# A two-layer relational graph network: copying two tiles of rows in every eighth chunk instead of every sixteenth

## The chip, the cores and the metric

The kernel runs on one core of a Trainium2 chip. Its engines are TensorE (PE, matrix products), VectorE (DVE), ScalarE (ACT), GpSimd (POOL) and SyncE (SP). ACT, POOL and SP each also have a queue in which they start memory transfers, written ACTq, POOLq and SPq in the profile. The metric is the time of one execution in microseconds, the median of several runs. Lower is better.

## The reference

There are 50,000 nodes with 128 features each and 850,000 edges, of which 50,000 go from a node to itself. The edges are sorted by the node that they end in. Each edge has one of 16 types, and each type's matrix is a mix of 8 basis matrices. Two layers of this kind run one after the other, then comes a residual and a normalisation:

```
def _rgcn_layer(h, src, dst, rel, basis, w_comp, loop_w, bias):
    W = jnp.einsum('rb,bio->rio', w_comp, basis)
    seg = dst.astype(jnp.int32) * N_REL + rel.astype(jnp.int32)
    agg = jax.ops.segment_sum(h[src], seg, num_segments=N_ENT * N_REL)
    agg = agg.reshape(N_ENT, N_REL, -1)
    msg = jnp.einsum('nri,rio->no', agg, W)
    out = msg + h @ loop_w + bias
    return jax.nn.relu(out)
...
x = _layernorm(x + layer2(layer1(x)), axis=-1)
```

For every edge the 128 numbers of its source node have to be fetched: `h[src]`. These are 512-byte rows at places that are known only when the kernel runs.

## The kernel before

**Chunks.** The 800,000 edges that are not self-loops are cut into 625 chunks of 10 tiles of 128 edges (`C`, `K`, `P`). The loop over `c` near line 1238 goes through the chunks, once for each layer. The rows of one tile come with one indirect transfer that GpSimd starts (`gather`, line 270): 128 rows into the 128 partitions of one slice of a buffer `g`. In layer 1 there are four buffers of ten tiles and the gathers of chunk c+2 are written beside the products of chunk c (`FETCH`). In layer 2 there are nine buffers (the later ones are named `d_r`, `k_loop`, `real_both`, `full` and `parts`), and the gathers of chunk c+7 stand there.

**Products.** VectorE makes a matrix `hot` for each chunk (lines 1099 and 1106) that says, for every edge, to which of the next 30 nodes and with which of the 8 basis weights it counts. TensorE multiplies the fetched tile with it into a bank of PSUM (line 1273), five tiles to a bank, and VectorE adds the bank to `ring` (line 1130), which holds the sums of three groups of 512 nodes. When a group is finished, ScalarE copies its sums out (`own`, line 915), TensorE multiplies them with the basis (line 919), ScalarE applies the relu (line 934), and the result is turned back and stored.

**The copied tiles.** Some tiles are not gathered by GpSimd. For a chunk in `copied_rows` the gather of tile 9 (`COPIED`) is left out, and SyncE or ScalarE fetches the 128 rows one by one with 128 direct transfers of 512 bytes. The class `Copied` does this. `load` fetches the 128 row addresses from DRAM (line 1181). `copy` loads 16 of them at a time into the engine's registers (line 1190, shown as TENSOR_LOAD; the 128th alone on line 1188), computes each address (line 1191, shown as FUSED_REGOPS or ISA) and starts the transfer (line 1192). Before the change each of the two engines does this for every sixteenth chunk (`EVERY`), with one buffer each.

**What sets the order.** Work that is not part of the chunk's own products stands in a list of events with a due time. One unit of due time, called a slot below, is one tile's product, so that a chunk is ten slots. `later(time, ...)` enters an event, and `go_on(now)` writes out what is due after each product. The rows of a copied tile are such events: `planned` spreads the 128 of them over a stretch of slots ahead of the chunk. TensorE takes the copied tile of chunk c at slot 10c+5, as the first tile of the second half. The engines PE, POOL, DVE and ACT execute in the order in which the program is written (line 1093). SP is not in that list before the change, so its order is chosen by the framework's scheduler.

**Semaphores of the transfers.** The transfers of SyncE and ScalarE together tell of their landing with eight semaphores, DMAHW0 to DMAHW7, which are handed out in turn. Each transfer waits until the one before it on the same semaphore has landed. That is the eighth transfer before it, counted over both queues.

Of the kernel before, what the change touches and what calls it, by code (L numbers as in the profile page):

```python
# [40 lines left out]
F32 = mybir.dt.float32  # L41
# [10 lines left out]
P = 128  # L52
# [4 lines left out]
K = 10  # L57
# [15 lines left out]
GATHERS = 4  # L73
J = 4
AHEAD = 16
EACH = 2 * len(WINDOWS)
NEAR = 128
BATCH = 4
# [9 lines left out]
WIDE = 1  # L88
PARTS_OF = ((0, 3), (3, 5))
EPS = 1e-5  # L90
EVERY = 16
COPIED = 9
EARLY = ((27, 35), (19, 27))
LEAD = 2
AT_A_TIME = 16

# [6 lines left out]
def tile_rgcn_resnorm(  # L103
# [55 lines left out]
    consts = ctx.enter_context(tc.tile_pool(name="consts", bufs=1))  # L159
    col = consts.tile([P, P], F32, name="col")  # L160
    nc.gpsimd.iota(col, pattern=[[1, P]], base=0, channel_multiplier=0, allow_small_or_imprecise_dtypes=True)
    part = consts.tile([P, 1], F32, name="part")
    nc.gpsimd.iota(part, pattern=[[0, 1]], base=0, channel_multiplier=1, allow_small_or_imprecise_dtypes=True)
    ident = consts.tile([P, P], F32, name="ident")
    nc.vector.tensor_scalar(ident, col, part, None, op0=OP.is_equal)

    single = consts.tile([P, 4], F32, name="single")
    eps, apart_by, odd, ones = (single[:, i : i + 1] for i in range(4))
    nc.vector.memset(eps, EPS)

# [12 lines left out]
    def weighed(brief):  # L183
# [19 lines left out]
        for n, (basis, w_comp, loop_w, bias) in enumerate(GIVEN):  # L203
            ec = brief.tile([P, NB], F32, name="ec")
            nc.scalar.dma_start(
                ec, bass.AP(tensor=w_comp.tensor, offset=w_comp.offset, ap=[[0, AT], [NB, NR], [1, NB]])
            )
            nc.vector.tensor_tensor(
                each[:, n],
                ec[:, None, :].to_broadcast([P, AT, NB]),  # L210
                one_tile[:, :, None].to_broadcast([P, AT, NB]),
                op=OP.mult,
            )

            column_of = consts.tile([P, 1], F32, name=f"bias_of{n}")
            nc.scalar.dma_start(column_of, bass.AP(tensor=bias.tensor, offset=bias.offset, ap=[[1, P], [1, 1]]))
            BIAS_OF.append(column_of)
            left, mine = ec, brief.tile([P, NB], F32, name="mine")
            for i in range(PARTS):
                short = brief.tile([P, NB], BF16, name=f"short{i}")  # L220
                nc.vector.tensor_copy(short, left)
                if i == 0:
                    nc.vector.tensor_scalar(mine, short, which[:, i : i + 1], None, op0=OP.mult)
                else:
                    nc.vector.scalar_tensor_tensor(
                        mine, short, which[:, i : i + 1], mine, op0=OP.mult, op1=OP.add
                    )
                if i + 1 < PARTS:
                    less = brief.tile([P, NB], F32, name=f"less{i}")
                    nc.vector.tensor_tensor(less, left, short, op=OP.subtract)  # L230
                    left = less
            nc.vector.tensor_copy(split[:, n], mine)
# [483 lines left out]
    def chunked():  # L716
        with (
# [334 lines left out]

            def indexed(n, b, copy):
                first_of, end_of = b * AHEAD * K, min(C, (b + 1) * AHEAD) * K
                index[n, b] = hp.tile([P, AHEAD * K], I32, name="index", bufs=3)
                return copy(index[n, b][:, : end_of - first_of], src[:, first_of:end_of])

            placed = indexed(0, 0, nc.vector.tensor_copy)
# [31 lines left out]
                for who, engine in enumerate((nc.sync, nc.scalar))  # L1090
            ]
            ordered = ExitStack()
            ordered.enter_context(tc.manual_schedule(engines={mybir.EngineType.PE, mybir.EngineType.Pool, mybir.EngineType.DVE, mybir.EngineType.Activation}))
            for n, of in enumerate((x, H1)):

                def hot_of(c):
# [17 lines left out]
                def places(c):  # L1114
                    loaded_for[0] = n, c // BATCH
                    some = min(BATCH, C - c) * EACH
                    which_of = c % AHEAD // BATCH * BATCH * EACH
                    nc.vector.load(at_reg[:some], offs[c // AHEAD][0:1, which_of : which_of + some])

                def add(c, half, i, pa):  # L1120

# [30 lines left out]
                offs = {}  # L1152

                def offsets(b):
                    first_of, end_of = b * AHEAD * EACH, min(C, (b + 1) * AHEAD) * EACH
                    offs[b] = hp.tile([1, AHEAD * EACH], I32, name="offs")
                    nc.sync.dma_start(
                        offs[b][:, : end_of - first_of], OFF[first_of:end_of].rearrange("(p k) o -> p (k o)", p=1)
                    )
# [12 lines left out]
                class Copied:  # L1172
# [3 lines left out]
                        self.order = [*range(1, P), 0]  # L1176

                    def load(self):
                        self.to = hp.tile([P, D], F32, name=f"copied{self.who}", bufs=1)
                        self.away = self.to.bitcast(I32)[0:1, :]  # L1180
                        nc.sync.dma_start(self.away, AWAY[2 * self.c + 1 : 2 * self.c + 2])

# [12 lines left out]
                        )  # L1195

                    def planned(self, queue):
                        begin = K * (self.c - EVERY + LEAD) + PER
                        queue(begin - K, self.load)
                        for i in range(P):  # L1200
                            queue(begin + i * (EVERY - 2 * LEAD) * K // P, self.copy, i)

                copied_rows = {
                    c: Copied(c, who) for who, early in enumerate(EARLY[n]) for c in range(early, C, EVERY)
# [4 lines left out]
                batches = [Weights(c, n) for c in range(0, C, BATCH)]  # L1209
                batches[0].load()  # L1210
                offsets(0)
                for b in range(1, -(-C // AHEAD)):
                    later(K * AHEAD * b - K, offsets, b)
                if n == 0:
                    batches[0].compare()
                    batches[0].multiply()
# [13 lines left out]
                for one in groups:  # L1230
                    free = one.planned(later, free)
                if n:
                    with tc.issue_after(back[0].ins):
                        matrices(1, nc.sync)

                into = rows + more_rows(pr) if n else rows
                ahead = FETCH[n]
# [272 lines left out]
```

## Time and profile before

| | |
|---|---|
| median of 3 runs | 15,544.52 us (15,542.33 to 15,545.87) |
| the profiled execution | 15,567.63 us; span from the first to the last instruction 15,565.8 us |
| busy: PE / DVE / ACT / POOL | 62% / 50% / 11% / 75% of the span |
| POOL instructions | 12,390 |
| copied tiles | 151: 76 by SyncE, 75 by ScalarE |
| memory traffic | 98 GB/s over the span, DMA engines about a third busy |

The page of the profile gives busy time by engine, the span in 40 slices, the chain of work that ended last, and groups of instructions. A group's row names the line, the engine, the operation and the tiles, then after the bar its busy time in us, the mean of one in ns, and the idle time of the engine just ahead of it. A trace can be asked further for one tile's or line's instructions (shortest, median and longest in ns), for who waited for whom (us in total, times, longest), for stretches of time, and for the instructions in order of time.

### The profile page before, as it was taken

To read this page: it belongs to the slowest core of one execution; us is meant where nothing else is said; L and a number is where in the kernel's file an instruction comes from. 1 tells how busy PE (TensorE), PEld (TensorE's weight loads), DVE (VectorE), ACT (ScalarE), POOL (GpSimd) and SP (SyncE) were. 2 spreads that over 40 slices of the span, in tenths; PEclk is the share of its full clock that TensorE was granted. 3 is DMA by queue.
4 is the path that set the end of the run, shared out by engine and by line. 5 is a ranking of instruction groups with operands and counts; after the bars stand their busy time and mean duration, and the time that the engine had idled before them with its cause. 6 is when DMAs were issued, how large, how long until landed. Compare 5 with 4: busy or idle time off the path is not lost.

```text
span 15565.8 us, 164019 instructions
## 1 busy us (share of the span) xinstructions
PE 9727.8 (62%) x31567; PEld 7176.4 (46%) x31567; DVE 7738.2 (50%) x11079; ACT 1642.8 (11%) x2031; POOL 11742.7 (75%) x12390
## 2 busy tenths in 40 slices
PE   5666566666666666666666666666666666666666
PEld 4444444444444444444444444444444444444444
DVE  7655555565444444444444444444444444444444
ACT  1111111111111111111100000000000000000000
POOL 7777777777777777777777777777777777777777
PEclk7877887777888888888877777787777777777778
DMA  4333333333333333333333333333333333333332
GB/s 125 109 111 107 109 110 106 107 106 105 99 99 96 99 99 98 98 99 98 94 92 94 94 94 94 93 92 93 94 94 94 94 94 94 92 94 94 94 94 81
DMA packets 827507, 1530.93 MB, mean 98 GB/s; under 512 B 245150, under 2 KB 332937, under 8 KB 826472
## 3 DMA queue, kind: packets, MB, share of 16 engines
q0 software_dynamic: 397104, 817.16, 18.8%
q1 hardware_dynamic: 408424, 697.64, 13.4%
q10 hardware_dynamic: 20944, 5.55, 0.2%
q14 instruction: 778, 6.37, 0.1%
q8 instruction: 257, 4.21, 0.1%
HBM read 1391.28 MB, written 128.09 MB: 98 GB/s over the span
## 4 chain that ended last, share of the span: by engine, by line
POOL 61%; issue 24%; DMA 11%; PE 2%; DVE 1%; SPq 1%; ACTq 0%; ACT 0%; POOLq 0%; DVEq 0%
POOL g L270 43%; DMA g<-in_x_dram,index 5%; POOL d_r L270 4%; POOL k_loop L270 4%; POOL parts L270 4%; POOL full L270 4%; POOL real_both L270 3%; DMA g<-H,index 2%; PE pa L1273 1%; DMA real_both<-H,index 1%; DMA full<-H,index 1%; DMA k_loop<-H,index 1%; DMA parts<-H,index 1%; DMA d_r<-H,index 1%; SPq L1190 0%
## 5 line engine op out<-in xcount | busy, mean ns | idle before, releaser
L1273 PE MATMUL pa<-hot,g 128*128 128x240 f32 x17882 | 5490.0, 459 | 4012.8 <-DMA g<-in_x_dram,index 2195.9
L270 POOL DMA_INDIRECT g<-in_x_dram,index x6175 | 5875.3, 951 | 1890.1 <-issue 1783.7
L1273 PEld LDWEIGHTS pa<-hot,g 128*128 128x128 f32 x17882 | 4155.0, 242 | 5580.4 <-issue 2374.8
L1130 DVE TENSOR_TENSOR ring<-pa,ring 128x240 f32 x5000 | 2038.6, 408 | 7077.2 <-PE pa L1273 6275.3
L1106 DVE TENSOR_TENSOR hot<-pm,fixed 128x2400 f32<-128x2400 f32 x1250 | 3317.9, 2654 | 69.7 <-ACT pm L789 17.4
L270 POOL DMA_INDIRECT g<-H,index x2766 | 2616.6, 946 | 857.1 <-issue 814.1
L919 PE MATMUL pn<-own,basis 128*128 128x512 f32 x3072 | 1808.1, 674 | 0.0
L900 DVE TENSOR_TENSOR ring<-wide,pa 128x2048 f32<-128x2048 f32 (+1 forms) x386 | 876.4, 2270 | 230.8 <-DMA wide<-CW 212.2
L915 ACT COPY own<-ring 128x4096 f32<-128x4096 f32 x192 | 692.3, 3606 | 2444.1 <-DVE ring L1130 1100.6
L270 POOL DMA_INDIRECT k_loop<-H,index x682 | 645.2, 946 | 208.1 <-issue 197.4
L270 POOL DMA_INDIRECT real_both<-H,index x682 | 645.3, 946 | 208.0 <-issue 194.3
L270 POOL DMA_INDIRECT d_r<-H,index x682 | 645.2, 946 | 208.0 <-issue 198.6
L270 POOL DMA_INDIRECT parts<-H,index x681 | 644.3, 946 | 207.8 <-issue 197.4
L270 POOL DMA_INDIRECT full<-H,index x681 | 644.2, 946 | 207.8 <-issue 194.7
L919 PEld LDWEIGHTS pn<-own,basis 128*128 128x128 f32 x3072 | 667.3, 219 | 65.5
L1273 PE MATMUL pa<-hot,real_both 128*128 128x240 f32 x1364 | 445.4, 482 | 334.7 <-DMA real_both<-H,index 317.0
L1273 PE MATMUL pa<-hot,k_loop 128*128 128x240 f32 x1364 | 442.6, 479 | 318.7 <-DMA k_loop<-H,index 287.3
L1273 PE MATMUL pa<-hot,full 128*128 128x240 f32 x1362 | 444.3, 481 | 310.5 <-DMA full<-H,index 292.3
L1273 PE MATMUL pa<-hot,d_r 128*128 128x240 f32 x1364 | 442.6, 479 | 311.7 <-DMA d_r<-H,index 275.2
L1273 PE MATMUL pa<-hot,parts 128*128 128x240 f32 x1362 | 444.4, 481 | 304.1 <-DMA parts<-H,index 268.6
L887 ACT COPY pa<-hT 128x512 f32<-128x512 f32 x392 | 228.8, 587 | 3534.0 <-DMA copied<-H 1798.0
L1099 DVE TENSOR_TENSOR fixed<-fixed,key 128x300 f32<-128x300 f32 x1250 | 584.5, 468 | 1.6
(181 smaller groups left out, 5255.8 us busy)
## 6 DMA issues: line engine op xcount, KB each, us to landing
wide<-CW SPq DMA_DIRECT2D x388, 1024.0 KB
g<-in_x_dram,index POOLq DMA_INDIRECT x6175
copied<-in_x_dram SPq DMA_DIRECT2D x4864, 0.5 KB
copied<-H SPq DMA_DIRECT2D x4864, 0.5 KB
copied<-H ACTq DMA_DIRECT2D x4864, 0.5 KB
copied<-in_x_dram ACTq DMA_DIRECT2D x4736, 0.5 KB
rows<-in_x_dram SPq DMA_DIRECT2D x194, 256.0 KB
g<-H,index POOLq DMA_INDIRECT x2766
```

The source lines that it names most:

```text
L270: return nc.gpsimd.indirect_dma_start(out=to, out_offset=None, in_=of, in_offset=bass.IndirectOffsetOnAxis(ap=idx, axis=0))
L887: nc.scalar.copy(self.laid[b][:, : self.cnt], self.hT[:, : self.cnt])
L900: nc.vector.tensor_tensor(into, wide, laid[:, None, :].to_broadcast([P, AT_ONCE, cnt]), op=OP.mult)
L915: nc.scalar.copy(self.sums, ring[:, :, at : at + cnt])
L919: nc.tensor.matmul(self.pn[:, a:e], BASIS[:, b, :], self.sums[:, b, a:e], start=False, stop=b == NB - 1)
L1099: nc.vector.tensor_tensor(own, grid[:, None, :].to_broadcast([P, K, WN]), key[:, c * K : (c + 1) * K, None].to_broadcast([P, K, WN]), op=O ...
L1106: nc.vector.tensor_tensor(hot, pm[:, c % BATCH * K * NB : (c % BATCH + 1) * K * NB].rearrange("e (k b) -> e k b", b=NB)[:, :, :, None].to_ ...
L1130: nc.vector.tensor_tensor(into, pa[:, before : before + NB * w].rearrange("d (b w) -> d b w", w=w), into, op=OP.add,)
L1273: nc.tensor.matmul(pa[:, before : before + NB * w], fetched, hot[:, half * PER + j].rearrange("e b w -> e (b w)"), start=(i, j) == mine[i][0],
```

## The change

Each engine now copies a tile for every eighth chunk (`EVERY` 8). SyncE starts at chunk 20 in layer 1 and 12 in layer 2, ScalarE four chunks later. Each has two buffers in place of one. The 128 copies of a tile are spread over 80 slots, from slot 10(c-9)+5 to slot 10(c-1)+5; before they were spread over 120 slots, from 10(c-14)+5 to 10(c-2)+5. SyncE's transfers stand in the written order, since SP joins the list of engines with a manual schedule. To make room in SBUF, `index` has two buffers instead of three, the offsets of eight chunks are loaded at once instead of sixteen, and a few one-column constants share a tile. The load of the second layer's matrices no longer names a transfer that it is to follow.

```
+PLACED = 8
...
-EVERY = 16
+EVERY = 8
 COPIED = 9
-EARLY = ((27, 35), (19, 27))
+EARLY = ((20, 24), (12, 16))
...
-                index[n, b] = hp.tile([P, AHEAD * K], I32, name="index", bufs=3)
+                index[n, b] = hp.tile([P, AHEAD * K], I32, name="index")
...
-            ordered.enter_context(tc.manual_schedule(engines={mybir.EngineType.PE, mybir.EngineType.Pool, mybir.EngineType.DVE, mybir.EngineType.Activation}))
+            ordered.enter_context(tc.manual_schedule(engines={mybir.EngineType.PE, mybir.EngineType.Pool, mybir.EngineType.DVE, mybir.EngineType.Activation, mybir.EngineType.SP}))
...
-                    first_of, end_of = b * AHEAD * EACH, min(C, (b + 1) * AHEAD) * EACH
-                    offs[b] = hp.tile([1, AHEAD * EACH], I32, name="offs")
+                    first_of, end_of = b * PLACED * EACH, min(C, (b + 1) * PLACED) * EACH
+                    offs[b] = hp.tile([1, PLACED * EACH], I32, name="offs")
...
-                        self.to = hp.tile([P, D], F32, name=f"copied{self.who}", bufs=1)
+                        self.to = hp.tile([P, D], F32, name=f"copied{self.who}")
...
-                        begin = K * (self.c - EVERY + LEAD) + PER
+                        begin = K * (self.c - EVERY - LEAD + 1) + PER
                         queue(begin - K, self.load)
                         for i in range(P):
-                            queue(begin + i * (EVERY - 2 * LEAD) * K // P, self.copy, i)
+                            queue(begin + i * EVERY * K // P, self.copy, i)
...
-                for b in range(1, -(-C // AHEAD)):
-                    later(K * AHEAD * b - K, offsets, b)
+                for b in range(1, -(-C // PLACED)):
+                    later(K * PLACED * b - 2 * K, offsets, b)
...
-                    with tc.issue_after(back[0].ins):
-                        matrices(1, nc.sync)
+                    matrices(1, nc.sync)
```

(`tc.manual_schedule` keeps the written order on the engines named. The pool `hp` has two buffers where none is named.)

The first place is on POOL, early in layer 1. Each row is one chunk's gathers, with the count behind the x. Before:

```order
L270 DMA g_102<-in_x_dram,index 128x128 x9
L270 DMA g_99<-in_x_dram,index 128x128 x10
L270 DMA g_100<-in_x_dram,index 128x128 x10
L270 DMA g_101<-in_x_dram,index 128x128 x10
L496 DMA FULL<-full,to_i 1638400x2
L270 DMA g_102<-in_x_dram,index 128x128 x10
L270 DMA g_99<-in_x_dram,index 128x128 x10
L270 DMA g_100<-in_x_dram,index 128x128 x10
L270 DMA g_101<-in_x_dram,index 128x128 x10
L270 DMA g_102<-in_x_dram,index 128x128 x9
```

And with the change (its lines are one further down):

```order
L271 DMA g_98<-in_x_dram,index 128x128 x9
L271 DMA g_99<-in_x_dram,index 128x128 x10
L271 DMA g_100<-in_x_dram,index 128x128 x10
L271 DMA g_101<-in_x_dram,index 128x128 x10
L271 DMA g_98<-in_x_dram,index 128x128 x9
L271 DMA g_99<-in_x_dram,index 128x128 x10
L271 DMA g_100<-in_x_dram,index 128x128 x10
L497 DMA FULL<-full,to_i 1638400x2
L271 DMA g_101<-in_x_dram,index 128x128 x10
L271 DMA g_98<-in_x_dram,index 128x128 x9
```

A chunk with nine gathers comes every fourth chunk instead of every eighth. No other POOL instruction moves.

The second place is on SP, in the middle of layer 1, with the semaphores that each row waits for in brackets. L1190 loads sixteen addresses, L1192 starts one row's transfer, and L1191 between them computes the address. Before:

```order
L1192 DMA copied_25547<-in_x_dram 1x128 [waits DMAHW0_49]
L874 DMA wide<-CW 128x4x512 [waits DMAHW1_49,DVE_49]
L755 DMA rel<-REL 128x1x640 [waits DMAHW2_49,DVE_49]
L1191 ISA
L1192 DMA copied_25547<-in_x_dram 1x128 [waits DMAHW3_49]
L1191 ISA
L1192 DMA copied_25547<-in_x_dram 1x128 [waits DMAHW4_49]
L1191 ISA
L1192 DMA copied_25547<-in_x_dram 1x128 [waits DMAHW5_49]
L1191 ISA
L1192 DMA copied_25547<-in_x_dram 1x128 [waits DMAHW6_49]
L1181 DMA copied_26377<-AWAY 1x128 [waits DMAHW7_49,Activation_sequencer_49,PE_49]
```

And with the change, where the same three lines are L1191, L1193 and L1192:

```order
L1193 DMA copied_35952<-in_x_dram 1x128 [waits DMAHW6_49]
L1192 ISA
L1193 DMA copied_35952<-in_x_dram 1x128 [waits DMAHW0_49]
L1192 ISA
L1193 DMA copied_35952<-in_x_dram 1x128 [waits DMAHW2_49]
L1192 ISA
L1193 DMA copied_35952<-in_x_dram 1x128 [waits DMAHW4_49,SP_sequencer_49]
L1191 TENSOR_LOAD copied_37159 [waits DMAHW5_49]
L1192 ISA
L1193 DMA copied_37159<-in_x_dram 1x128 [waits DMAHW5_49]
L1192 ISA
L1193 DMA copied_37159<-in_x_dram 1x128 [waits DMAHW6_49]
```

Before, SP's rows here take the eight semaphores one after the other, so that the transfers between are its own. With the change they take every second one, the others going to ScalarE's rows, and the next tile's load of addresses follows directly on the last row of the tile before.

More of the change, by code (lines that the diff above doesn't have):

```diff
@@ L161, in tile_rgcn_resnorm @@
     nc.gpsimd.iota(col, pattern=[[1, P]], base=0, channel_multiplier=0, allow_small_or_imprecise_dtypes=True)
-    part = consts.tile([P, 1], F32, name="part")
+    single = consts.tile([P, 8], F32, name="single")
+    part = single[:, 4:5]
     nc.gpsimd.iota(part, pattern=[[0, 1]], base=0, channel_multiplier=1, allow_small_or_imprecise_dtypes=True)
@@ L165, in tile_rgcn_resnorm @@
     nc.vector.tensor_scalar(ident, col, part, None, op0=OP.is_equal)
-    single = consts.tile([P, 4], F32, name="single")
     eps, apart_by, odd, ones = (single[:, i : i + 1] for i in range(4))
@@ L213, in weighed @@
             )
-            column_of = consts.tile([P, 1], F32, name=f"bias_of{n}")
+            column_of = single[:, 5 + n : 6 + n]
             nc.scalar.dma_start(column_of, bass.AP(tensor=bias.tensor, offset=bias.offset, ap=[[1, P], [1, 1]]))
```

4 lines of the change are left out of this document (2 added, 2 removed).

## Prediction

> **What bounds the kernel now.** I read the page first: the chain that ended last, then GpSimd's group.
>
> ```profile
> POOL 61%; issue 24%; DMA 11%; PE 2%; DVE 1%; SPq 1%; ACTq 0%; ACT 0%; POOLq 0%; DVEq 0%
> L270 POOL DMA_INDIRECT g<-in_x_dram,index x6175 | 5875.3, 951 | 1890.1 <-issue 1783.7
> ```
>
> The chain is GpSimd's. One gather takes 951 ns and 0.306 us of idle time stand ahead of it, nearly all "issue", which means that it waits for nobody. Then I read stretches of time, one in each layer:
>
> ```profile
> core 0: us, PE busy (x) PEld busy (x) DVE busy (x) ACT busy (x) POOL busy (x), PEclk, DMA share, GB/s
> 5000.00:6000.00 1000.00, 632.76 (x2151) 476.25 (x2150) 463.38 (x555) 113.87 (x136) 755.91 (x800) 0.81 0.33 98
> 11000.00:13000.00 2000.00, 1261.99 (x3790) 912.63 (x3788) 934.66 (x1317) 192.27 (x239) 1512.23 (x1600) 0.78 0.31 94
> ```
>
> GpSimd issues 800 gathers in 1000 us and 1600 in 2000 us: one every 1.250 us, without a pause. No other engine is busy for more than two thirds. There are 2 x 625 x 10 - 151 = 12,349 gathers (the 151 copied tiles are the row of line 1181 below), and 12,349 x 1.250 = 15,436 us. The remaining 130 us of the span are the start, the turn between the layers and the end. A chunk takes 15,436 / 1250 = 12.35 us. In the list of waits there is no row in which PE waits for a copied tile, so today the copies arrive in time.
>
> **What the change removes.** Copied tiles in layer 1: SyncE for chunks 20, 28, ... 620 and ScalarE for 24, ... 624, 76 each. In layer 2: 12, ... 620 and 16, ... 624, 77 each. Together 306, which is 155 more than 151. So 155 gathers go, and if GpSimd stays the bound this is worth 155 x 1.250 = 194 us. Nothing hides them. A chunk would then have 9.75 gathers and take 12.19 us.
>
> **What it adds: 155 x 128 rows on two queues.** Each queue must now deliver 16 rows in each chunk's 12.19 us, all the time. Before it was 16 rows in 1.5 chunks, with a pause of four chunks after each tile. So the question is what 16 rows cost a queue. The copied tile's instructions (shortest/median/longest in ns):
>
> ```profile
> L1192 SPq DMA_DIRECT2D copied<-in_x_dram x4864: 224/228/922, 123.5 to 7688.8; - x195
> L1190 SPq TENSOR_LOAD <-copied x608: 3257/3524/5519, 119.4 to 15326.6; - x152
> L1190 ACTq TENSOR_LOAD <-copied x600: 3212/3738/6103, 304.4 to 15425.0; - x150
> L1188 SPq TENSOR_LOAD <-copied x76: 447/538/806, 247.5 to 15341.3; - x76
> L1181 SPq DMA_DIRECT2D copied<-AWAY x151: 215/231/867, 110.2 to 15287.0; - x151
> ```
>
> 608 loads for 76 tiles are eight for a tile, one for each 16 rows, and one costs the queue 3.5 us (SP) or 3.7 us (ACT). The Trainium skill, in "DMA: Bandwidth & Descriptors", section "Latency and other measured facts", gives a floor of about 600 ns for such a register load; the row for one register (538 ns) agrees, but by that figure alone for 16 registers a batch would be 2.9 us cheaper, the queues would have room to spare and the change would bring its 194 us. The measured load of 16 decides against it.
>
> The pace of rows, from stretches without a wait, in order of time (start, us, ... xcount):
>
> ```profile
> 5058.66 1.46 SPq L1192 DMA_DIRECT2D copied<-in_x_dram  x4
> 5060.22 0.40 SPq L874 DMA_DIRECT2D wide<-CW  x1
> 5060.82 2.69 SPq L1192 DMA_DIRECT2D copied<-in_x_dram  x7
> ```
>
> ```profile
> 5146.71 1.00 ACTq L1192 DMA_DIRECT2D copied<-in_x_dram  x3
> ```
>
> SP: (1.46 - 0.228) / 3 = 0.411 us a row. ACT, with the same 0.23 us for the last: (1.00 - 0.23) / 2 = 0.385 us. Another transfer between SP's rows (`wide`) stretches the gap from 5060.12 to 5060.82, 0.70 us where 0.18 us is usual: its own 0.40 us and 0.12 us around it.
>
> So 16 rows without any wait cost SP 3.52 + 16 x 0.411 + about 0.1 behind the load, and an eighth of the single load (0.08): **10.3 us**. ACT: 3.74 + 16 x 0.385 + 0.2 = 10.1 us, and 0.3 us as an estimate for handing on its own 1.6 instructions a chunk (239 in 2000 us above).
>
> SP also carries all other transfers:
>
> ```profile
> L874 SPq DMA_DIRECT2D wide<-CW x392: 364/399/447, 99.2 to 15445.9; - x196
> L824 SPq DMA_DIRECT2D lrel<-LREL x98: 641/672/692, 81.2 to 7594.8; - x98
> L755 SPq DMA_DIRECT2D rel<-REL x157: 582/629/757, 20.9 to 7689.1; - x157
> L936 SPq DMA_DIRECT2D H1T<-oT x98: 319/354/862, 217.8 to 7815.6; - x98
> ```
>
> In layer 1 there are 196 `wide`, 98 `lrel`, 157 `rel`, four more kinds of 98 and one of 157 at about 0.354, and with the change 152 + 79 short ones at 0.23: 78 + 66 + 99 + 139 + 56 + 53 = 491 us, and 1,231 x 0.12 = 148 us around them: 639 us over 625 chunks, **1.02 us a chunk**. Layer 2 has no `lrel`, `rel` or `CW`: 196 `wide`, three kinds of 98 and one of 157, 154 + 79 short ones, by the same sum 0.64 us.
>
> SP's queue is thus taken for 11.3 of 12.19 us in layer 1 and for 10.9 in layer 2. What is left for waits is 0.9 and 1.3 us a chunk.
>
> **What waits cost.** Each transfer waits for the eighth before it. SP's own list of waits, for the rows alone (us, times, longest):
>
> ```profile
> SPq L1192 <- DMA wide<-CW: 278.3, 98, 4.8
> SPq L1192 <- DMA copied<-in_x_dram: 195.7, 150, 6.3
> SPq L1192 <- DMA copied<-H: 169.5, 179, 4.6
> SPq L1192 <- DMA lrel<-LREL: 55.0, 24, 4.7
> SPq L1192 <- DMA rows<-in_x_dram: 38.9, 32, 5.4
> SPq L1192 <- DMA out_dram<-t: 10.2, 6, 1.8
> ```
>
> Layer 1 has `in_x_dram`, `lrel`, `rows` and half of `wide`: 429 us over its 304 loads, 1.41 us for 16 rows. Layer 2: 319 us, 1.05 us. By these, SP needs 12.7 us a chunk in layer 1, over the 12.19, and 12.0 in layer 2, just under.
>
> The two queues also stop each other, since they share the eight semaphores:
>
> ```profile
> 5124.22 21.09 ACTq L1192 DMA_DIRECT2D copied<-in_x_dram  x16
> ```
>
> ```profile
> 5140.09 0.36 SPq L831 DMA_DIRECT2D rows<-in_x_dram  x1
> ```
>
> These 16 rows of ScalarE took 21.1 us instead of 10.1, and they went on when SyncE had issued its `rows`. That one was SyncE waiting for an engine, which goes away when the queues lag. The part that stays is that with both queues always copying, the eight transfers between are four of each: 4 x 0.411 = 1.64 us, where SP alone has 8 x 0.411 = 3.3. No view gives this part. Below it is 0: each queue's waits fall together. Above, a load of one queue (3.5 us) lets the other go on for eight rows at most, 8 x 0.385 = 3.1 us; losing 0.4 us at each of two loads a batch is 0.8 us. I take 0.3, nearer the lower end since most waits are for `wide` and `lrel`, which hold both queues at once.
>
> **The sum.** Layer 1: 11.3 + 1.4 + 0.3 = 13.0 us a chunk against 12.35: 625 x 0.65 = +406 us. Layer 2: 10.9 + 1.05 + 0.3 = 12.25, against 12.35: -62 us. When the copies are late, PE waits at slot 10c+5 of the copied chunk, its buffers stay full, and GpSimd waits for a buffer: three chunks of gathers ahead cover a single delay, but not a queue that is too slow on average. The profiled time of 15,568 becomes 15,912; the median shown lies 23 us below the profiled execution, so I say **15,890 us**.
>
> The other edits cost nothing that I can find: the written order on SP puts every transfer at its due slot, 10 to 60 slots ahead of its use; `index` is rewritten only when its gathers lie seven chunks or more back; 39 more loads of offsets a layer are in the sum.
>
> **Rivals.** (A) The waits fall where a queue is ahead and would wait anyway; GpSimd stays the bound. For it: no PE wait for a copied tile today, and ten slots (12 us) between the last row's due slot and its use. Against: the queues are 90% taken before any wait. Then 15,545 - 194 = **15,350 us**. (B) The queues run at about today's chunk, 12.35 us on average: no change, 15,545. (C) The forecast: the row copies of SyncE bound layer 1. (D) Full coupling: 0.8 instead of 0.3 us, 13.5 and 12.75 us a chunk, 625 x (1.15 + 0.40) = +970 us, **16,510 us**. It decides as soon as one queue's load regularly stops the other. (E) SyncE, now in written order, stops at a transfer whose data are not there, and rows queue behind it; each such stop over the slack of 12 us would cost its excess. Today's largest sum of that kind is
>
> ```profile
> SPq L1181 <- PE pa L1273: 1812.3, 142, 27.7
> ```
>
> 12.8 us on average, for a buffer that PE has yet to free; with two buffers it was freed a whole tile earlier, so I count this rival to D.
>
> **How the numbers follow.** A 0.35, B 0.06, C 0.42, D and E 0.17. A measurement of this kernel can tell 0.2% (31 us) from no change. Faster is A, slower is C, D and E: 0.35, 0.06, 0.59. The forecast is C's. C's own range, with 0 to 0.6 us of coupling (12.7 to 13.3 and 12.19 to 12.55 us a chunk), is 15,660 to 16,260. The range that holds 8 in 10 reaches from A's full gain to D: 15,340 to 16,450.
>
> **What would show it.** If C is right, the waits of the profile have a new row "PE pa <- DMA copied", GpSimd issues fewer than 800 gathers in 1000 us in layer 1 (about 750) but near 800 in layer 2, GpSimd's idle time is ended by PE, and SP's queue in layer 1 has next to no waits for other engines left. If A is right, 800 in both, and PE never waits for `copied`. If layer 2 is as slow as layer 1, it is D. I would be wrong altogether if a row's transfer or a load took a different time at twice the density; the medians of lines 1191 and 1193 would show it.

## The result and the profile after

The changed kernel takes 16,392.78 us (16,383.57 to 16,406.22) against 15,544.97 us beside it. The ratio is 1.0546, with an interval from 1.0528 to 1.0565. It is slower by 848 us where the prediction said 345. The time lies inside the range of 15,340 to 16,450 us, but above the range of the forecast's own theory C, 15,660 to 16,260. The profiled execution took 16,406.22 us (span 16,404.4), 839 us over that of the kernel before.

Where the time went is read first. The first fence is the answer for the tile `g` on GpSimd, in the kernel before: shortest, median and longest gather in ns, then the first and the last start in us.

```profile
L270 POOL DMA_INDIRECT g<-in_x_dram,index x6175: 943/947/2332, 18.8 to 7805.6; - x200
L270 POOL DMA_INDIRECT g<-H,index x2766: 943/947/1044, 7820.2 to 15543.1; - x198
```

The second is the same for the changed kernel, whose lines are one further down.

```profile
L271 POOL DMA_INDIRECT g<-in_x_dram,index x6098: 938/945/1997, 18.8 to 8609.7; - x197
L271 POOL DMA_INDIRECT g<-H,index x2731: 940/945/1183, 8664.6 to 16304.2; - x196
```

Layer 2 begins at 7,820.2 us before and at 8,664.6 us after, so layer 1 lost 844 us. Layer 2 takes 15,565.8 - 7,820.2 = 7,746 us before and 16,404.4 - 8,664.6 = 7,740 us after: its 77 fewer gathers brought nothing that shows. A gather itself is as long as it was.

The chain that ended last and three groups of the changed kernel (busy us, mean ns, then idle us ahead and who ended most of it):

```profile
SPq 34%; DMA 28%; issue 13%; ACTq 12%; POOL 5%; DVE 3%; PE 3%; ACT 1%; DVEq 0%; POOLq 0%
L271 POOL DMA_INDIRECT g<-in_x_dram,index x6098 | 5789.9, 949 | 2675.7 <-issue 1793.1
L1273 PE MATMUL pa<-hot,copied 128*128 128x240 f32 x612 | 277.0, 546 | 1802.0 <-DMA copied<-H 1000.0
L901 DVE TENSOR_TENSOR ring<-wide,pa 128x2048 f32<-128x2048 f32 (+1 forms) x386 | 880.3, 2281 | 3531.9 <-DMA wide<-CW 3453.3
```

GpSimd's share of the chain fell from 61% to 5%; in its place stand the two copying queues and their transfers. PE's products with a copied tile, which had nobody to wait for, now have 1,802 us of idle time ahead of them. VectorE now waits 3,453 us for `wide`, the 1 MB transfers on SyncE's queue; it was 212 us before. Whether that is a second cause is taken up with the experiment without them. The list of waits (us, times, longest) has PE's waits for the rows and GpSimd's for PE:

```profile
PE pa L1273 <- DMA copied<-H: 1000.0, 116, 25.9
POOL g L271 <- PE pa L1273: 823.9, 170, 31.1
PE pa L1273 <- DMA copied<-in_x_dram: 461.5, 59, 25.5
```

PE waits for rows that are not there, in both layers, and GpSimd waits for buffers that PE has not emptied. Now the stretches of time:

```profile
core 0: us, PE busy (x) PEld busy (x) DVE busy (x) ACT busy (x) POOL busy (x), PEclk, DMA share, GB/s
5000.00:6000.00 1000.00, 537.61 (x1976) 412.95 (x1977) 420.21 (x505) 104.85 (x121) 677.05 (x718) 0.77 0.32 89
11000.00:13000.00 2000.00, 1038.52 (x3776) 811.84 (x3775) 926.77 (x1305) 191.85 (x237) 1511.71 (x1601) 0.75 0.33 95
```

In layer 1 GpSimd issues 718 gathers in 1000 us. In layer 2 it issues 1,601 in 2000 us, its full pace. Yet layer 2 is no shorter. The second number misleads: with nine buffers GpSimd runs ahead of PE, and PE gets through a chunk no faster than the copies come. After the last gather at 16,304.2 us the kernel needs another 100 us, where the kernel before needed 23.

The copied tile's instructions give the pace of the copies (shortest/median/longest ns, first and last start):

```profile
L1193 SPq DMA_DIRECT2D copied<-H x9856: 224/228/361, 8703.0 to 16340.2; - x198
L1193 SPq DMA_DIRECT2D copied<-in_x_dram x9728: 224/228/776, 191.3 to 8600.4; - x199
L1191 SPq TENSOR_LOAD <-copied x1224: 3074/3524/4523, 187.6 to 16330.2; - x175
L1191 ACTq TENSOR_LOAD <-copied x1224: 3212/3724/6455, 243.5 to 16367.8; - x175
```

9,728 rows are 608 batches of 16, one for each chunk: (8,600.4 - 191.3) / 608 = **13.83 us a batch in layer 1**, and (16,340.2 - 8,703.0) / 616 = **12.40 us in layer 2**. The chunk before took 12.35 us. No single transfer or load became longer than before; the time stands between them. SyncE's own list of waits shows it:

```profile
SPq L1193 <- DMA copied<-H: 681.0, 603, 4.3
SPq L1193 <- DMA copied<-in_x_dram: 655.5, 618, 22.4
SPq L1193 <- DMA wide<-CW: 348.3, 98, 7.5
SPq L1193 <- DMA rows<-in_x_dram: 227.4, 85, 6.6
SPq L1191 <- DMA copied<-in_x_dram: 106.4, 69, 3.6
SPq L1193 <- DMA lrel<-LREL: 78.8, 19, 5.2
SPq L875 <- DVE pa L898: 47.6, 6, 21.2
```

Waits for rows (`copied`) were 195.7 us in layer 1 over 304 batches; they are 655.5 us over 608, one stop of 1.06 us in each batch. The large waits for engines, 1,812 us at the load of addresses alone, are gone; the largest one left is the 47.6 us of the last row. The same list, asked for 400 to 8,600 us, adds up to 1,458 us of waits for transfers and 30 us for engines. That is 17.8% and 0.4% of the stretch, so of the 13.83 us of a batch in layer 1 about 2.5 us are waits and 11.3 us issue. From 8,710 to 16,300 us it is 1,014 and 43 us, 13.4% and 0.6%: 1.7 us of waits and 10.7 us of issue in layer 2. SyncE hardly waits for an engine in either layer, so no engine holds up its queue.

### The profile page after: what moved, and what is told of

The parts are those of the page before. It is cut to its first block, busy times and chain, and to the rows that moved or that the text cites. A ratio compares the mean times of both kernels' runs of the same rounds, so it can differ in the third digit from the quotient of the medians.

```text
span 16404.4 us, 225255 instructions
## 1 busy us (share of the span) xinstructions
PE 8856.9 (54%) x31567; PEld 6825.5 (42%) x31567; DVE 7748.5 (47%) x11079; ACT 1657.0 (10%) x2031; POOL 11574.7 (71%) x12235
## 4 chain that ended last, share of the span: by engine, by line
SPq 34%; DMA 28%; issue 13%; ACTq 12%; POOL 5%; DVE 3%; PE 3%; ACT 1%; DVEq 0%; POOLq 0%
SPq L1193 15%; SPq L1191 15%; DMA wide<-CW 11%; DMA copied<-in_x_dram 7%; ACTq L1191 6%; DMA copied<-H 6%; ACTq L1193 5%; POOL g L271 3%; SPq L1192 2%; PE pa L1273 2%; DMA lrel<-LREL 1%; DVE ring L1131 1%; DMA rows<-in_x_dram 1%; ACT own L916 1%; DVE hot L1107 1%
## 5 line engine op out<-in xcount | busy, mean ns | idle before, releaser
L271 POOL DMA_INDIRECT g<-in_x_dram,index x6098 | 5789.9, 949 | 2675.7 <-issue 1793.1
L1273 PE MATMUL pa<-hot,g 128*128 128x240 f32 x17658 | 4920.9, 433 | 3084.6 <-DVE ring L1131 1535.6
L1273 PEld LDWEIGHTS pa<-hot,g 128*128 128x128 f32 x17658 | 3985.3, 231 | 4421.0 <-DVE ring L1131 1679.0
L920 PE MATMUL pn<-own,basis 128*128 128x512 f32 x3072 | 1691.2, 634 | 0.0
L1273 PE MATMUL pa<-hot,copied 128*128 128x240 f32 x612 | 277.0, 546 | 1802.0 <-DMA copied<-H 1000.0
L1273 PEld LDWEIGHTS pa<-hot,copied 128*128 128x128 f32 x612 | 132.4, 258 | 1945.8 <-DMA copied<-H 741.4
L768 DVE TENSOR_TENSOR is_rel<-fixed,rel 128x640 f32<-128x640 f32 (+1 forms) x157 | 129.4, 824 | 1266.4 <-DMA rel<-REL 1266.4
L920 PEld LDWEIGHTS pn<-own,basis 128*128 128x128 f32 x3072 | 627.2, 206 | 52.4
L1273 PE MATMUL pa<-hot,parts 128*128 128x240 f32 x1346 | 375.9, 431 | 255.8 <-DVE ring L1131 198.3
L1273 PE MATMUL pa<-hot,full 128*128 128x240 f32 x1346 | 372.5, 428 | 255.8 <-DVE ring L1131 213.4
```

Of the source, the lines that this page charges most:

```text
L271: return nc.gpsimd.indirect_dma_start(out=to, out_offset=None, in_=of, in_offset=bass.IndirectOffsetOnAxis(ap=idx, axis=0))
L920: nc.tensor.matmul(self.pn[:, a:e], BASIS[:, b, :], self.sums[:, b, a:e], start=False, stop=b == NB - 1)
L1273: nc.tensor.matmul(pa[:, before : before + NB * w], fetched, hot[:, half * PER + j].rearrange("e b w -> e (b w)"), start=(i, j) == mine[i][0],
```

## The experiments

The theory after the result: SyncE's queue sets the pace of layer 1, and its batch is longer than the sum said because the two queues' rows stop each other on the eight semaphores (W). Rivals: SyncE's own issue and its waits for its own large transfers are enough (S); layer 2's depth of buffers or PE's is short (B); the written order is to blame; VectorE's waiting for `wide` is a cause of its own. "Control" is the changed kernel again, beside the first group of experiments.

### The changed kernel again

No edit.

> The changed kernel as it is, as a control beside the others of this call. On a chip where the kernel before takes about 15,545 us: 16,390 us, a ratio of 1.055. On a chip where the kernel before takes about 20,000 us, because the queues stall at their own instructions: SyncE's and ScalarE's queues have twice the instructions of before, so if those stalls grow with the number of instructions (theory F, fetch) the ratio is well over 1.055, about 1.2; if the chip is only slower as a whole, 1.055.

Measured: 16,424.21 us, 1.0574 (1.0544 to 1.0605) of the kernel before, which took 15,531.56 us there. The loss stands. The kernels below are compared with it.

### Fewer buffers in layer 2

```
-FETCH = (2, 7)
+FETCH = (2, 2)
...
-                into = rows + more_rows(pr) if n else rows
+                into = rows
```

> The changed kernel with layer 1's four gather buffers and two chunks of lead in layer 2 as well. Theory S (SyncE's queue sets layer 1's pace since it has more transfers there and longer waits): layer 2 keeps its pace of the control, since SyncE's queue there needs no more than before, within 1% of the control. Theory B (four buffers cannot cover late copies): layer 2 falls to layer 1's pace, about 650 to 900 us over the control.

Measured: 16,467.69 us, 1.0602 (1.0571 to 1.0633), 43 us over the control, within the 1% that S gave; B's 650 to 900 us did not come. The stretch in layer 2:

```profile
11000.00:13000.00 2000.00, 1035.86 (x3750) 808.19 (x3750) 923.14 (x1301) 188.11 (x235) 1471.51 (x1560) 0.75 0.33 93
```

With four buffers GpSimd cannot run ahead, and its pace falls from 1,601 gathers to 1,560 in 2000 us: 9.75 gathers then take 12.50 us, near SyncE's 12.40 us a batch. So layer 2 was bound by the copies as well, and the five further buffers hide only a delay of some chunks.

### The density of before in layer 1, the new one in layer 2

```
-EVERY = 8
+EVERY = ((16, 16), (8, 8))
...
-EARLY = ((20, 24), (12, 16))
+EARLY = ((28, 36), (12, 16))
```

(`EVERY` is then read by layer and engine; the written order on SP and all else of the change stay.)

> The changed kernel with both engines copying every sixteenth chunk in layer 1, spread over 160 slots with two buffers, and every eighth in layer 2. Theory S: SyncE's queue is half empty in layer 1, which runs at GpSimd's 9.875 x 1.25 = 12.34 us as before, and layer 2 at 12.2: 15,545 - 97 = 15,450 us, a ratio of 0.994. If the new order or the buffers cost something by themselves, layer 1 is slower than before: over 15,600 us.

Measured: 15,560.40 us, 1.0019 (1.0007 to 1.003). All of the loss is gone, so it is the density in layer 1 that costs it. But the gain of layer 2 did not come. Its waits say why:

```profile
PE pa L1273 <- DMA copied<-H: 993.8, 117, 26.8
POOL g L271 <- PE pa L1273: 31.0, 34, 5.3
L1193 SPq DMA_DIRECT2D copied<-H x9856: 224/228/591, 7852.5 to 15506.7; - x198
```

(The third row is from the tile's instructions.) PE waits 993.8 us for the copied rows of layer 2, and the batch takes (15,506.7 - 7,852.5) / 616 = 12.43 us. GpSimd hardly waits, and that is no proof of a gain.

### SyncE's tiles alone

```
-                    c: Copied(c, who) for who, early in enumerate(EARLY[n]) for c in range(early, C, EVERY)
+                    c: Copied(c, who) for who, early in enumerate(EARLY[n]) for c in range(early, C, EVERY) if who == 0
```

> The changed kernel, where only SyncE copies tiles (the 153 of its list; those of ScalarE are gathered by GpSimd again). No transfer of ScalarE's rows then stands between SyncE's on the shared semaphores. W (SyncE is late because the two queues stop each other): SyncE's batch of 16 rows falls from 13.8 us in layer 1 to at most 12.3, GpSimd sets the pace again with 9.875 gathers a chunk, 12.34 us, and the time is within 0.3% of before, 15,500 to 15,580. S (SyncE's own issue and its waits for its own and the other small transfers are enough to make it late): the batch stays at 13.2 us or more and the time at 16,000 or more.

Measured: 15,621.6 us, 1.006 (1.0043 to 1.0077): 800 us under the control, and 40 us over the upper end that W gave.

```profile
L1193 SPq DMA_DIRECT2D copied<-in_x_dram x9728: 224/228/858, 191.9 to 7812.9; - x199
L1191 SPq TENSOR_LOAD <-copied x1224: 3074/3523/5780, 188.2 to 15513.0; - x175
```

SyncE does the same work with the same loads, and its batch in layer 1 falls from 13.83 to (7,812.9 - 191.9) / 608 = 12.53 us. Its waits at rows:

```profile
SPq L1193 <- DMA wide<-CW: 433.5, 194, 4.6
SPq L1193 <- DMA lrel<-LREL: 241.9, 73, 4.5
SPq L1193 <- DMA rows<-in_x_dram: 37.0, 87, 1.0
SPq L1191 <- DMA copied<-in_x_dram: 23.1, 20, 1.6
```

The two large rows for `copied` are gone: among eight transfers that are all its own, no row waits for another row, only 23.1 us of loads do. Of 12.53 us, 11.4 are issue and 1.15 are waits. So ScalarE's rows on the shared semaphores cost SyncE **1.3 us a batch**. W holds for the main part.

Rows that merely land later would give such waits too, and the two traces can tell the one from the other. From a row's issue to the last count on its semaphore, its landing, the median for SyncE's rows in layer 1 is 1.51 us with both queues and 1.44 us with SyncE alone: they land about as fast. But eight of SyncE's rows in a row take 8 x 0.411 = 3.3 us until the semaphore comes round, and four only 1.64 us, which leaves hardly more than the landing. And of the 649 us that rows of SyncE waited for rows between 400 and 8,600 us of the changed kernel, 534 us, in 414 stops, were for a row that ScalarE had started. In the kernel before it was 137 of 196 us.

A small part of S stays: 12.53 us is 0.2 us more than the 12.34 us of 9.875 gathers, and PE still waits 346 us in layer 1.

### Half of each register load

```
-                            if some[-1] == 0:
-                                self.engine.load(self.at[AT_A_TIME - 1 :], self.away[:, 0:1])
-                                some = some[:-1]
-                            self.engine.load(self.at[: len(some)], self.away[:, some[0] : some[-1] + 1])
-                        at = self.engine.snap(self.at[i % AT_A_TIME], min_val=0, max_val=(N - 1) * D)
+                            self.engine.load(self.at[: AT_A_TIME // 2], self.away[:, some[0] : some[0] + AT_A_TIME // 2])
+                        at = self.engine.snap(self.at[i % AT_A_TIME // 2], min_val=0, max_val=(N - 1) * D)
```

> The changed kernel, where a batch of 16 rows loads 8 addresses and uses each twice, so the copied tiles hold wrong rows and the output is wrong; all transfers stay. A load costs some 1.8 us instead of 3.5. If the queues' own issue lies on the path that sets the end, as the sum had it, a chunk of layer 1 falls from 13.8 to about 12.2 us and layer 2 to GpSimd's 12.2: 15,350 to 15,500. If the shorter load only gives more time to waits for the eight transfers before (latency bound), the chunk falls by less than half of that: 16,000 or more.

Measured: 15,463.99 us, 0.9957 (0.994 to 0.9973).

```profile
L1190 SPq DMA_DIRECT2D copied<-in_x_dram x9728: 224/228/928, 188.8 to 7738.8; - x199
L1188 SPq TENSOR_LOAD <-copied x1224: 1677/1925/3015, 186.7 to 15358.7; - x175
SPq L1190 <- DMA copied<-in_x_dram: 870.9, 718, 6.0
```

The load is 3,524 - 1,925 = 1,599 ns shorter, and the batch of layer 1 is 13.83 - 12.42 = 1.41 us shorter ((7,738.8 - 188.8) / 608 = 12.42). The queue's own issue therefore lies on the path almost in full; the waits for rows grew from 655.5 to 870.9 us, 0.35 us a batch, and took back the rest, while other waits became a little shorter. Layer 2 is now faster than GpSimd needs, and the 77 gathers saved there come through. The Trainium skill says in "Runtime: NRT & Kernel Launch", section "Instruction fetch mechanics", that a register load takes about 200 ns for each register, in bulk too. The trace agrees nearly: 3,524 / 16 = 220 ns and 1,925 / 8 = 241 ns.

### Without the `wide` transfers

The first `wide` tile is kept and used for every group, in place of 392 transfers of 1 MB.

```
+                    if kept_wide:
+                        self.wide[b] = kept_wide[0]
+                        return
...
+                    kept_wide.append(self.wide[b])
```

> The changed kernel without the wide transfers after the very first (392 of 1 MB; the sums of the groups are scaled with the wrong weights). Theory S: SyncE's queue loses 0.31 x 0.52 = 0.16 us of issue a chunk and the waits for wide, 0.3 us of its own and about as much over ScalarE, so layer 1 goes from 13.8 to about 13.1 us and the time falls by 350 to 450 us against the control. Theory W (VectorE's 3,453 us of waiting for wide, which SyncE issues late, set the pace): layer 1 goes to GpSimd's 12.2 us, 900 us less than the control.

Measured: 15,673.57 us, 1.0091 (1.0062 to 1.012), 751 us under the control: between the two expectations, nearer the one called W here. (In this expectation W is VectorE's waiting for `wide`, not the waiting of the two queues for each other, which is W in the other parts.)

```profile
L1198 SPq DMA_DIRECT2D copied<-in_x_dram x9728: 224/228/780, 186.9 to 7943.9; - x199
SPq L1198 <- DMA copied<-in_x_dram: 222.9, 492, 3.0
SPq L1198 <- DMA lrel<-LREL: 211.6, 51, 6.2
```

The batch of layer 1 is (7,943.9 - 186.9) / 608 = 12.76 us. The issue of 196 transfers with the 0.12 us around each is 196 x 0.52 / 625 = 0.16 us a chunk, but 1.07 us went. The rows' waits for `copied` fell to a third. So the wait for a 1 MB transfer and the waits of the queues for each other are not two separate terms of a sum: with `wide` gone, the queues also stop each other for less. The trace of the changed kernel agrees: of the 534 us that SyncE's rows waited for ScalarE's in layer 1, 316 us were for rows started within 7 us after a `wide`, which itself lands 6.2 us after its issue (median). The slowest tenth of ScalarE's rows takes 3.6 us or more to land there, and 2.0 us or more without `wide`.

VectorE's waiting is not the cause, although the time came near that expectation. Layer 1 did not go to GpSimd's 12.2 us, and SyncE waited for engines in only 0.4% of layer 1 of the changed kernel, so VectorE does not hold its queue. With half of each register load all `wide` transfers are still there, and VectorE's waits for them fall from 3,453 to 1,108 us:

```profile
DVE ring L901 <- DMA wide<-CW: 1108.0, 208, 13.3
```

With every tenth chunk they are 211 us. So VectorE waits for `wide` because SyncE's queue is late, and not the other way round.

### The order on SP

```
-            ordered.enter_context(tc.manual_schedule(engines={mybir.EngineType.PE, mybir.EngineType.Pool, mybir.EngineType.DVE, mybir.EngineType.Activation, mybir.EngineType.SP}))
+            ordered.enter_context(tc.manual_schedule(engines={mybir.EngineType.PE, mybir.EngineType.Pool, mybir.EngineType.DVE, mybir.EngineType.Activation}))
```

> The changed kernel with SyncE's queue ordered by the scheduler, as before the change, in place of the written order. If the written order is what makes SyncE late, the time falls by 300 us or more. If it is the amount of rows alone, the time stays within 100 us of 16,424; if the order of before makes SyncE stop for engines with rows queued behind it, it rises above 16,500.

Measured: 16,327.78 us, 1.0513 (1.0495 to 1.053). The loss stays, so the order is not its cause. Against the control's 1.0574 (1.0544 to 1.0605) the scheduler's order is even some 95 us better, just at the edge of what was given for "the amount alone". Layer 1 has nearly the same length: the second layer begins at 8,673 us, against 8,665 us in the result's trace and 8,684 us in the control's. Layer 2 takes 7,655 us where the control's takes 7,747. The batch of layer 2 is (16,265.2 - 8,677.7) / 616 = 12.32 us instead of 12.40, with shorter waits for rows:

```profile
SPq L1193 <- DMA copied<-in_x_dram: 650.4, 592, 21.8
SPq L1193 <- DMA copied<-H: 502.1, 508, 4.2
L1193 SPq DMA_DIRECT2D copied<-H x9856: 224/228/377, 8677.7 to 16265.2; - x198
```

### Every tenth chunk

```
-EVERY = 8
+EVERY = 10
...
-EARLY = ((20, 24), (12, 16))
+EARLY = ((22, 27), (14, 19))
```

> The changed kernel with every tenth chunk in place of every eighth for both engines: 244 copied tiles. By the after trace SyncE's 16 rows cost 13.8 us in layer 1 and 12.4 in layer 2, and now have 1.25 chunks, 15.4 us, so it is not late; GpSimd has 12,500 - 244 gathers at 1.250 us, 93 fewer than before: 15,545 - 116 = 15,430, range 15,400 to 15,480. If a queue's rows are late for a reason other than the average pace, the time is above 15,530 in spite of that room.

Measured: 15,435.05 us against 15,529.45, 0.9938 (0.9922 to 0.9955). This is the fastest of the kernels that compute the whole.

```profile
L1193 SPq DMA_DIRECT2D copied<-in_x_dram x7808: 224/228/962, 191.3 to 7721.3; - x196
PE pa L1273 <- DMA copied<-in_x_dram: 6.9, 4, 4.7
11000.00:13000.00 2000.00, 1256.87 (x3826) 917.73 (x3827) 944.36 (x1333) 192.65 (x242) 1511.44 (x1603) 0.79 0.33 94
```

A batch has 1.25 chunks, and (7,721.3 - 191.3) / 488 = 15.43 us is 1.25 times 12.34: here GpSimd leads and the copies follow. PE waits for copied rows 6.9 us in the whole kernel. 93 gathers fewer than before are 93 x 1.250 = 116 us by the forecast's price; 94 us came.

### The same kernels where the kernel before takes 20,000 us

In three groups of runs the kernel before itself took 20,213, 19,961 and 19,968 us, on three chips, of which one gave 15,530 us at other times. These runs can only be compared with the kernel before beside them. Among them is ScalarE's share alone:

```
+                    c: Copied(c, who) for who, early in enumerate(EARLY[n]) for c in range(early, C, EVERY) if who == 1
```

> The changed kernel with the tiles of ScalarE alone (153); SyncE only carries the other transfers. Theory S: SyncE's queue is nearly empty, ScalarE needs 10.4 us and waits of 1 to 1.5 us, under the 12.34 us of GpSimd: 15,545 us, the time before, within 0.5%. If ScalarE's queue is as full as SyncE's, or ScalarE's own work is held back by its rows: 15,800 us or more.

What was expected of the order on SP, half loads and SyncE's tiles alone ahead of these runs, and of every tenth chunk:

> The changed kernel with SyncE's transfers in the scheduler's order again; everything else as changed. Theory S (SyncE's queue is full: 11.4 us of issue and some 2.4 us of waits for 16 rows in layer 1, whatever the order): about 16,390 us, within 1.5%, and layer 1 at about 706 gathers in 1000 us. Theory O (the written order lets the wide and rel transfers stand behind rows, and VectorE waits for them): under 15,700 us, with layer 1 near 800 gathers in 1000 us.

> The changed kernel with 8 addresses loaded for 16 rows, each used for two rows, so half the copied rows are wrong and half of the register loads' time is gone. Theory S: SyncE's queue falls from 13.8 by half a load, 1.8 us, to 12.0 us a chunk in layer 1, under the 12.19 us of GpSimd, so 15,350 to 15,500 us. Theory B (layer 1 has too few buffers for late copies) and theory O: the rows come no less late behind the other work, over 16,000 us. Theory L (the shared semaphores hold SyncE's queue, not its issue): most of the 850 us stays, about 16,200 us.

> The changed kernel with the tiles of SyncE alone (153 of them, every eighth chunk); ScalarE's 153 tiles are gathered by GpSimd again, so a chunk has 9.875 gathers, 12.34 us. Theory S: SyncE still needs 11.4 us and its waits for 16 rows, with waits of about 1.4 us since the semaphores are its own: 12.8 us in layer 1, 12.34 in layer 2, about 15,850 us. Theory L (ScalarE's rows cost SyncE more than 1.5 us a chunk over the semaphores): 12.34 us in both, 15,545 us.

> The changed kernel with a tile of each engine in every tenth chunk (244 tiles, 93 more than before). SyncE needs 12.8 rows a chunk: 0.8 x 10.4 = 8.3 us of rows and loads, 1.1 us of other transfers, 0.8 x 2.4 = 1.9 us of waits, 11.3 us in layer 1, under GpSimd's 9.8 x 1.25 = 12.25 us. So the whole gain: 15,531 - 93 x 1.25 = 15,415 us, a ratio of 0.9925. If the waits do not shrink with the density, 8.3 + 1.1 + 2.9 = 12.3: no change, 1.000.

| kernel | us | ratio to the kernel before |
|---|---|---|
| ScalarE's tiles alone | 22,197.58 | 1.0982 (1.0949 to 1.1016) |
| SyncE's tiles alone | 23,111.41; again 22,900.82 | 1.1435 (1.1401 to 1.1468); 1.1474 (1.1441 to 1.1506) |
| every tenth chunk | 22,428.69 | 1.1239 (1.1218 to 1.1261) |
| half loads | 23,879.93; 23,604.0; 23,587 | 1.1815 (1.1758 to 1.1871); 1.1824 (1.177 to 1.1877); 1.1818 (1.1792 to 1.1843) |
| order on SP by the scheduler | 25,138.32; 24,891 | 1.2437 (1.2401 to 1.2473); 1.2471 (1.2423 to 1.2519) |

Every kernel that adds copied rows is slower here, also the one that is faster elsewhere, and none of the expectations in us applies. The rows that differ are those of the queues' plainest instruction, the move of an address. SyncE's tiles alone, first here and then where the kernel before takes 15,529 us:

```profile
L1193 SPq MOVE copied<-in_x_dram x9728: 1/29/1452, 220.8 to 11527.6; - x199
```

```profile
L1193 SPq MOVE copied<-in_x_dram x9728: 29/29/43, 191.9 to 7812.8; - x199
```

A move that takes 29 to 43 ns there takes up to 1,452 ns here. More below.

## Why the prediction missed, step by step

**The bound before and its prices held.** GpSimd's 1.250 us a gather is met wherever the copies are on time (1,603 gathers in 2000 us with every tenth chunk). The 194 us for 155 gathers was of the right kind: with the copies in time, 93 gathers fewer gave 94 us where 116 was due.

**The issue of SyncE was right.** The sum had 11.3 and 10.9 us a chunk; the trace after has 11.3 and 10.7. That it lies on the path is shown by the half loads, where 1.41 of 1.60 us came back. (The load of a single register took 538 ns in the median and 447 ns at the least, so the floor of about 600 ns that the prediction found to agree is met only roughly.)

**The step that failed is "What waits cost"**, there the sentence "I take 0.3, nearer the lower end". It made 1.41 + 0.3 = 1.7 us a batch in layer 1; the trace after has 2.5. The mechanism of theory C was right, and this term was too small. SyncE alone has 1.15 us of waits, a little under the 1.41, and ScalarE's company adds 1.3 us in all, more than even the upper bound of 0.8. Counted by the layers' lengths, layer 1 lost 844 us where 406 was forecast, which is 438 of the 494 us by which the profiled time missed its forecast of 15,912. (The 0.83 us between 13.83 and 13.0 would make 625 x 0.83 = 519; but layer 1 before took 7,801 / 625 = 12.48 us a chunk with its start and the turn, which the sum left at 12.35.)

Of the 0.8 us that were missing, some 0.3 us stood ahead of rows and 0.5 us ahead of loads and of SyncE's other transfers. Three things were wrong inside that step. The upper bound let the queues stop each other only at the two register loads. But the trace has one stop for another row in each batch, 1.06 us on average (655.5 / 618), and `wide` makes these stops longer, as its removal shows: they fell to 222.9 us. Next, the 1.41 us came from a list that held only waits ahead of rows. Waits ahead of loads (106.4 us, 0.17 us a batch) and ahead of SyncE's other transfers (0.28 us a batch) were left out. And the argument for the lower end, "most waits are for `wide` and `lrel`, which hold both queues at once", was the wrong reading of that list: with half of `wide`, as the prediction itself counts it, `wide` and `lrel` have 194 of the 429 us of layer 1, and copied rows as much, 195.7 us. The two queues' rows waited for rows before the change too, although they overlapped only part of the time; SyncE alone has no such row. The full overlap should have been priced from that row.

**Layer 2** was forecast at 12.25 us a chunk and a gain of 62 us; it is 12.40 us and 6 us. The term is again the waits: 1.05 + 0.3 = 1.35 assumed, 1.7 measured. Here the error in the sum is smaller partly by luck, since the issue had been put 0.2 us too high.

**The rivals.** A (the copies hide) and B (no change) fell. D (full coupling) was the nearest in time, 16,510 us against 16,393, but its prices were 13.5 and 12.75: layer 1 is above it and layer 2 below it, and its sign, a second layer as slow as the first, did not appear. E, where SyncE stops at a transfer whose data are not there, has no support: the waits of SyncE for engines all but vanished, as the forecast C had it.

**The signs.** The new waits of PE for `copied`, GpSimd's idle time ended by PE and the missing engine waits of SyncE came as said. "About 750" gathers in 1000 us of layer 1 were 718. "Near 800 in layer 2" came too, and was a bad sign to choose: behind nine buffers GpSimd's pace shows nothing of PE's until they are full, as the run with four buffers shows.

**The other edits** were put at nothing. Of these the written order on SP costs some 90 us in layer 2, by one comparison; the rest was not tried apart.

## What to carry to other kernels

Before work is moved to a queue that waits for its own earlier transfers, measure the pace of the whole batch on that queue, with the other queue busy as it will be, and leave it room: here 16 rows, with what else the queue carries, took 13.8 us where the issue of the rows alone is 10.3 us, and spreading them over 1.25 chunks instead of one turned a loss of 5.5% into a gain of 0.6%. Where two queues share a fixed set of semaphores, price the coupling from every wait of the one that names a transfer of the other, at whichever instruction it stands. And do not judge a producer by its rate when there are deep buffers behind it: look at who waits at the consumer, and at the tail after the producer's last instruction.

## What the runs showed of the hardware

Two things were not expected. The first is the coupling above: 128 small transfers a tile on one queue run at 12.53 us for 16, and at 13.83 us when another queue does the same beside it, without the issue or the loads becoming longer in the median; the rows land 1.51 us after their issue instead of 1.44.

The second is what happens where the kernel before takes about 20,000 us. GpSimd's gathers are not longer there (these are SyncE's tiles alone, first there and then where the kernel before takes 15,529 us):

```profile
L271 POOL DMA_INDIRECT g<-in_x_dram,index x6174 | 5841.4, 946 | 5373.4 <-PE pa L1273 2604.9
```

```profile
L271 POOL DMA_INDIRECT g<-in_x_dram,index x6174 | 5853.5, 948 | 1902.4 <-issue 1834.3
```

A gather takes 946 and 948 ns, and only the idle time between grew, most of it ended by PE. On SyncE's queue, in the order of time, one sees rows that stretch (start us, us, ... count):

```profile
5024.94 11.68 SPq L1193 DMA_DIRECT2D copied<-in_x_dram  x19
...
5040.02 20.39 SPq L1193 DMA_DIRECT2D copied<-in_x_dram  x9
```

19 rows take 11.68 us (19 x 0.411 = 7.8, and a load of 3.5), as usual, but nine take 20.39 us. In this trace 5,111 of SyncE's moves and address sums take over 0.3 us each, in the median 0.70 us, in runs of about ten; where the kernel before takes 15,530 us none does. With ScalarE's tiles alone, 4,719 of ScalarE's do the same and none of SyncE's. So in these runs a kernel seems to pay for the number of instructions on the queues that copy: with ScalarE's 153 tiles 10%, with SyncE's 14 to 15%, with both and the scheduler's order 24 to 25%. The Trainium skill says in "Runtime: NRT & Kernel Launch", section "Instruction fetch mechanics", that instructions are fetched ahead in blocks of 256 and that the cost of a block's boundary is mostly hidden. The traces at 15,530 us agree, with no move over 43 ns in the row above. Nor does the other trace point to the fetch: the slow instructions stand no nearer to the packets of the instruction queues than random moments do (13.9 us after the last packet in the median, against 13.7 us). The cause stays open. The unmodified changed kernel was not run under these conditions.
